# Node degrees from bfloat16 halves in four column tiles, in a four-layer graph network

## The chip, the cores and the metric

The kernel runs on one core of one Trainium2 chip. The metric is the time of one execution on the device in microseconds, the median of several runs. One profiled execution gives the trace that the views are read from.

## The reference

Four graph layers work on the same 2048x2048 adjacency of zeros and ones (with ones on its diagonal), each followed by a residual and a layer normalization over 64 features; the batch is 8. Cut to what matters here:

```python
deg = jnp.maximum(adj.sum(-1), 1.0)[:, None]                       # layer 0
industry = jnp.einsum('nm,bmf->bnf', adj / deg, x @ W_ind)
...
A_td = A + jnp.eye(n); deg = jnp.sum(A_td, axis=1)                 # layer 1
A_hat = rsqrt(deg)[:, None] * A_td * rsqrt(deg)[None, :]
H = jnp.einsum('bmd,nm->bnd', X, A_hat)
```

Layer 0 also has an attention over hyperedges, mixed with `industry` by a second attention. Layers 2 (Chebyshev supports and a learned one) and 3 (three message steps) use the adjacency as it is.

## The kernel before, in words

The adjacency's transpose stays in SBUF for the whole run, as 16 tiles `adj[t]` of 128 rows in two halves of 1024 columns, marked float32r (a 32-bit word that TensorE takes in one pass). `adj_c(t, c)` is one of four chunks of 512 columns; chunks 0 and 1 lie in the left half, 2 and 3 in the right. POOL issues the loads (`load_adj`, L211): the left halves during the setup, the right halves two in each of the first eight slots of the slot stage (`to_load`, L787). The halves of tiles 0 to 6 and 15 are called adj in the profile, those of tiles 7 to 14 adj_more.

Products with the adjacency are 128x512 matmuls. The features are split into a rounded part and a rest (`v0h`, `v0l` and so on), so each product takes two. Features come as four pairs of batches p; g is the half of the columns. `products()` is a generator that issues one matmul (`ug`) and yields; after the pair p = 0, g = 0 it runs `degrees(0)` and `degrees(1)` (L346), 64 matmuls with a square of ones (`du`), which sum the columns; each is followed by a yield. `inverses()` then makes `dinv` and the inverse degrees from `deg4`.

This generator is the *filler*. `fill(n)` calls it n times between other work, so that TensorE has something to do there. First come the setup and 20 calls; then the **slot stage** (the attention over hyperedges): 16 tiles of nodes with 12, 5, 5, 4 and fewer slots each, 57 in all. A slot is three matmuls into `pz`, `fill(5)`, on VectorE L793, L797 and L802 with an exponential on ScalarE (L795) between the first two, and an addition on POOL (L803). `pz` has three buffers. Each tile but the last begins with `fill(3)` and the coefficients of the next one.

Then comes the **mix stage**, 16 steps of one pair and one chunk each. A step has scores (`pf`, four tanh), an end (`pt`, transposes of `ind`, then the normalization), `pi` and `pg` of the next step, and a weighing (`pd`, a tanh, then `ind` by L937), with a `fill` of 8 or 9 after each. When the products of layer 0 have run out, the filler goes on with `layer1(p)` (`u`). That needs its input as `part[p, c]`: chunk c of pair p has to be through its mix step and normalized, read back, scaled and cast. Until then the filler yields "wait": the call puts no matmul on TensorE and only advances the `tick` counters that place delayed work. After the mix stage there are 96 more calls around the preparation of layer 2 (`pb`), and a loop drains what the filler still has (L1134); then the learned support starts (`ua`).

Matmuls, the adjacency's loads and everything passed to `pin` keep their program order on their engine; the place of other instructions is chosen by a planner when the program is built.

In layer 3 `check()` (L1686) tests 64 times, one block of 128x512 each, whether the adjacency survived the rounding: ScalarE casts a block read anew from HBM (L1689), VectorE counts what differs (L1690). If anything was counted, a general kernel would run after this one.

Of the kernel before, what the change touches and what calls it, by code (L numbers as in the profile page):

```python
# [30 lines left out]
F32 = mybir.dt.float32  # L31
F32R = mybir.dt.float32r
BF16 = mybir.dt.bfloat16
# [4 lines left out]
ALU = mybir.AluOpType  # L38
# [18 lines left out]
def tile_gnn_fast(  # L57
# [24 lines left out]
    nc = tc.nc  # L82
# [3 lines left out]
    P = 128  # L86
    NT = N // P
    NP = B // 2
    C = 512
    NCH = N // C  # L90
# [8 lines left out]
    def cols(c, n=C):  # L99
        return slice(c * n, (c + 1) * n)  # L100
# [3 lines left out]
    def evacuate(dst, src):  # L104

        turn[0] ^= 1
        if turn[0]:
            nc.scalar.copy(dst, src)
        else:
            nc.vector.tensor_copy(dst, src)  # L110
# [60 lines left out]
    def mm(*args, **kw):  # L171
        tc.keep_in_program_order(nc.tensor.matmul(*args, **kw))  # L172

    def transpose(dst, src):
        tc.keep_in_program_order(nc.tensor.transpose(dst, src, ident))  # L175
# [6 lines left out]
    ones = const.tile([P, P], F32, name="ones")  # L182
# [17 lines left out]
    hy = hy_scope.enter_context(tc.tile_pool(name="hy", bufs=1))  # L200
# [12 lines left out]
    def adj_c(t, c):  # L213

        return adj[t][c // 2][:, cols(c % 2)]
# [3 lines left out]
        block = adj_c(t, t // JT)[:, cols(t % JT, P)]  # L219
        eng.tensor_tensor(block, block.bitcast(F32), ident, op)  # L220

    ones_r = hy.tile([P, P], F32R, name="ones_r")
    nc.vector.tensor_copy(ones_r, ones)
    number = hy.tile([P, 12], F32, name="number")
    for i in range(12):
        nc.gpsimd.memset(number[:, i:i + 1], -1.0 - i)
# [1 line left out]
    deg4 = hy.tile([P, C], F32, name="deg4")  # L228
# [82 lines left out]
    def later(n, f):  # L311

        pending.append([n, f])
# [7 lines left out]
    def tick():  # L321
        for e in pending + soon:
            e[0] -= 1
        while pending and pending[0][0] <= 0:
            pending.pop(0)[1]()
        for e in [e for e in soon if e[0] <= 0]:
            soon.remove(e)
            e[1]()
# [13 lines left out]
    def products():  # L342

        deg1 = hy.tile([P, NT], F32, name="deg1")

        def degrees(g):  # L346
            du = pph.tile([P, 2, C], F32, tag="ph", name=f"du{g}", bufs=2)
            for t in range(NT):
                for i in range(2):
                    mm(  # L350
                        du[:, i, :], lhsT=ones_r, rhs=adj_c(t, 2 * g + i), start=t == 0, stop=t == NT - 1
                    )
                    yield
            for i in range(2):
                c = 2 * g + i
                r = slice(c * P // NCH, (c + 1) * P // NCH)
                evacuate(deg4[r, :], du[r, i, :])

        def inverses():

            pdc = places["small"]([P, JT, P], "pdc")
            for j in range(JT):
                transpose(pdc[:, j, :], deg4[:, cols(j, P)])
            pdc = pdc.rearrange("p j (c r) -> p c j r", c=NCH)[:, :, :, 0]
            d1 = deg1.rearrange("p (c j) -> p c j", c=NCH)
            nc.vector.tensor_scalar(d1, pdc, 1.0, None, op0=ALU.add)
            nc.gpsimd.tensor_tensor(dinv, deg1, neg_half[:, :NT], ALU.pow)
            nc.vector.tensor_scalar(d1, pdc, 1.0, None, op0=ALU.max)
            nc.vector.reciprocal(deg1, deg1)
            for _ in range(20):  # L370
                yield
            for c in range(NCH):
                pt = places["small"]([P, C], "pinv")
                for j in range(JT):
                    k = c * JT + j
                    transpose(pt[:, cols(j, P)], deg1[:, k:k + 1].to_broadcast([P, P]))
                row = va.tile([P, C], F32, tag="ut", name="inv", bufs=2)
                nc.scalar.copy(row, pt)
                nc.sync.dma_start(inv_hbm[:, cols(c)], row)
                for _ in range(4):  # L380
                    yield

        for p in range(NP):
            for g in range(2):
                own = (2 * g, 2 * g + 1)
                ug = pph.tile([P, 2, C], F32, tag="ph", name="ug", bufs=2)
                u = {c: ug[:, c % 2, :] for c in own}
                turning = inverses() if p == 0 and g == 1 else iter(())
                for t in range(NT):
                    for i in range(2):  # L390
                        for c in own:
                            mm(
                                u[c], lhsT=part[t // JT][i][:, t % JT, :], rhs=adj_c(t, c),
                                start=t == 0 and i == 0, stop=t == NT - 1 and i == 1,
                            )
                            tick()
                            if t > 1:
                                next(turning, None)
                            yield
                    if p == NP - 1 and g == 1 and t % JT == JT - 1:  # L400
                        first_parts(t // JT, free)
                    if p + 1 < NP and t % JT == JT - 1:
                        c = t // JT
                        if g == 1:
                            parts(p + 1, c)
                        if g == 1 and c < 2 or g == 0 and c >= 2:
                            fetch(p + 1, (c + 2) % NCH)
                if p == NP - 1:

                    for t in range(g * NT // 2, (g + 1) * NT // 2):  # L410
                        onto_diagonal(t, nc.gpsimd, ALU.add)
                for c in own:
                    ut = va.tile([P, C], F32, tag="ut", name="ut", bufs=2)
                    nc.scalar.copy(ut, u[c])
                    nc.sync.dma_start(u0_hbm[p][:, cols(c)], ut)
                if p == 0 and g == 0:
                    yield from degrees(0)
                    yield from degrees(1)

    def fill(n):  # L420
        for _ in range(n):
# [12 lines left out]
    pph = ph_scope.enter_context(tc.tile_pool(name="ph", bufs=1, space=PSUM))  # L434
    with tc.tile_pool(name="pa_ps", bufs=1, space=PSUM) as pps:
# [60 lines left out]
        for b in range(2):  # L496
# [21 lines left out]
            flat, lhsT=tri, rhs=oh.rearrange("p t b -> p (t b)"), start=True, stop=False  # L518
        )
        for t in range(NT - 1):  # L520
            nc.tensor.matmul(
                flat[:, (t + 1) * BINS:], lhsT=ones_b,
                rhs=oh[:, t:t + 1, :].to_broadcast([P, NT - 1 - t, BINS]), start=False, stop=False,
            )
        nc.tensor.matmul(
            flat, lhsT=ones_b, rhs=gtb[:, None, :].to_broadcast(bins), start=False, stop=True
# [17 lines left out]
        for t in range(NT // 2):  # L544
            for k in range(2):
                r = slice(k * E, (k + 1) * E)
# [50 lines left out]
        for t in range(NT):  # L597
            ph = pph.tile([P, 2, C], F32, tag="ph", name="ph", bufs=2)
            for p in range(NP):
                nc.tensor.matmul(  # L600
                    ph[:, p // 2, (p % 2) * 2 * (F + 2):(p % 2 + 1) * 2 * (F + 2)], lhsT=xt[t][:, p, :],
                    rhs=bd66.rearrange("p b f -> p (b f)"), start=True, stop=True,
# [33 lines left out]
            for k in range(2):  # L636
                nc.tensor.matmul(
                    pagg[k * E:(k + 1) * E, 0:G * (F + 1)], lhsT=m_n[:, t, :], rhs=ex[:, k].rearrange("p g c -> p (g c)"),
                    start=t == 0, stop=t == NT - 1,
# [415 lines left out]
    for i in range(steps + 1):  # L1055
        k = 9 if i > NCH else 8
# [403 lines left out]
    h = [None] * NCH  # L1460
# [110 lines left out]
    h = [None] * NCH  # L1571
# [21 lines left out]
    for u in range(2, UNITS):  # L1593
        c, k = divmod(u, 2)
# [82 lines left out]
    left = l2.tile([P, NT, NCH], F32, tag="m", name="left")  # L1677
    left_d = l2.tile([P, NT], F32, name="left_d")
    checks = [(t, k) for t in range(NT) for k in range(NCH)]
    seen_a = fcav.rearrange("p i b f -> p (i b f)")  # L1680
# [5 lines left out]
    def check():  # L1686
        t, k = checks.pop(0)
        ar = va.tile([P, C], F32R, tag="ut", name="ar", bufs=2)
        nc.scalar.copy(ar, seen_a)  # L1689
        nc.vector.scalar_tensor_tensor(  # L1690
            ar.bitcast(F32), seen_a, 1.0, ar.bitcast(F32), op0=ALU.mult, op1=ALU.not_equal,
            accum_out=left[:, t, k:k + 1],
        )
        if t // JT == k:

            block = seen_a[:, cols(t % JT, P)]
            one, two, same = (ar[:, cols(i, P)] for i in range(3))
            nc.vector.tensor_tensor(one, block, ident, ALU.add)
            nc.vector.tensor_tensor(two.bitcast(F32), one.bitcast(F32), ident, ALU.subtract)
            nc.vector.scalar_tensor_tensor(  # L1700
                same.bitcast(F32), two.bitcast(F32), 1.0, block, op0=ALU.mult, op1=ALU.not_equal,
                accum_out=left_d[:, t:t + 1],
            )
        if checks:
            load_check()
        else:

            nc.vector.tensor_reduce(wrong[:, 4:5], left.rearrange("p t k -> p (t k)"), AX.X, ALU.add)
            nc.vector.tensor_reduce(wrong[:, 6:7], left_d, AX.X, ALU.add)
            nc.vector.tensor_reduce(total, wrong, AX.X, ALU.add)  # L1710

            def add_up():
                pl = lps.tile([1, 1], F32, tag="mm", name="pl", bufs=4)
                mm(pl, lhsT=total, rhs=ones[:, 0:1], start=True, stop=True)
                nc.vector.tensor_copy(bad, pl)

            later(40, add_up)
# [66 lines left out]
    for p in range(NP):  # L1784
# [3 lines left out]
        for step in range(STEPS):  # L1788
# [4 lines left out]
            for g in range(2):  # L1793
# [16 lines left out]
                for mine in ([[c] for c in own] if very_end else [own]):  # L1810
                    for t in range(NT if p or step else 0):
                        if checks and t in (2, 7, 12):
                            check()
                        for i in range(2):
                            for c in mine:
                                mm(
                                    u[c], lhsT=x_part[t // JT][i][:, t % JT, :], rhs=adj_c(t, c),
                                    start=False, stop=t == NT - 1 and i == 1,
# [15 lines left out]
        h = h_next  # L1834
# [749 lines left out]
```

## Time and profile before

| | |
|---|---|
| median of 3 runs | 1757.61 us (1756.46 to 1757.87) |
| the profiled execution | 1757.78 us, of which 1756.0 are the span of its instructions |
| mean granted TensorE clock | 0.982 |
| setup, to the first slot | to about 68 us |
| slot stage | about 68 to 225 us |
| mix stage | about 225 to 480 us |
| preparation of layer 2 and drain | to 516 us |
| layers 2 and 3 | to the end; layer 3's checks from 1319 to 1721 us |

The views are: busy time by engine, groups of instructions by line, the chain of waits that ended last, timelines of one engine, and busy time by stage. A line of a timeline has the start in us, the duration, the engine, the line of the kernel, the operation and its tiles, the count, and in brackets the idle time before it with its releaser. A matmul's duration there is its latency; what it costs in a row is the distance between starts.

### The profile page before, as it was taken

How to read it: one execution, taken by the hardware profiler on the slowest of the kernel's cores; microseconds unless marked ns; L12 is line 12 of the kernel's file. 1: busy time of each engine (PE TensorE's matmuls, PEld its weight loads, DVE VectorE, ACT ScalarE, POOL GpSimd, SP SyncE). 2: the span in 40 equal slices, each digit the busy share in tenths (PEclk: the TensorE clock that was granted, in tenths of full speed). 3: DMA queues.
4: the chain of work that ended last, by engine and by line, in shares of the span. 5: the costliest groups of instructions: out<-in, count | busy, mean ns of one | idle time of the engine just before them, and what ended most of it. 6: DMA issues, size and time to landing. Idle time of an engine off the chain costs nothing.

```text
span 1756.0 us, 28202 instructions
## 1 busy us (share of the span) xinstructions
PE 1670.1 (95%) x11196; PEld 1212.3 (69%) x11196; DVE 858.7 (49%) x1583; ACT 600.9 (34%) x1123; POOL 572.2 (33%) x515
## 2 busy tenths in 40 slices
PE   6889899999899999999999999999989999999996
PEld 4657666666664444478788877777767877878775
DVE  7678945778642221210146168888623433433332
ACT  1345533344222212112223178888502222222221
POOL 4578845556534443422023001313310200202001
PEclk9899999999999999999999999999999999999998
DMA  9744334444330000027244557675571111211211
GB/s 327 254 159 124 104 130 144 144 144 144 111 121 6 30 31 1 24 82 288 104 144 132 123 125 159 132 159 127 150 257 40 52 57 46 61 42 43 60 42 39
DMA packets 171182, 195.84 MB, mean 112 GB/s; under 512 B 71536, under 2 KB 116336, under 8 KB 169760
## 3 DMA queue, kind: packets, MB, share of 16 engines
q1 hardware_dynamic: 160096, 154.54, 30.3%
q0 software_dynamic: 8544, 30.68, 5.2%
q10 hardware_dynamic: 2400, 8.72, 1.4%
q8 instruction: 90, 1.47, 0.4%
q14 instruction: 52, 0.43, 0.1%
HBM read 126.72 MB, written 67.17 MB: 110 GB/s over the span
## 4 chain that ended last, share of the span: by engine, by line
PE 75%; DMA 4%; DVE 3%; POOL 2%; issue 2%; ACT 1%; SPq 1%; POOLq 0%; ACTq 0%; DVEq 0%
PE u L172 38%; PE ua L172 13%; PE py L172 7%; PE pw L172 5%; PE ug L172 3%; PE pr L172 2%; PE pf L172 1%; PE po L172 1%; PE pt L175 1%; DMA adj_more<-adj_hbm 1%; DVE w_half L1490 1%; PE s L172 1%; DMA est<-est_hbm 1%; PE pd L172 1%; PE pi L172 1%
## 5 line engine op out<-in xcount | busy, mean ns | idle before, releaser
L172 PE MATMUL ua<-pt,xn 128*128 128x512 f32 x512 | 230.2, 592 | 1.4 <-DVE pt L1150 1.4
L1488 ACT COPY w_half<-pw 128x512 f32<-128x512 f32 x316 | 191.5, 688 | 44.4 <-PE pw L172 43.4
L172 PEld LDWEIGHTS ua<-pt,xn 128*128 128x128 f32 x512 | 96.9, 190 | 111.1 <-issue 104.0
L1490 DVE COPY w_half<-pw 128x512 f32<-128x512 f32 x196 | 134.0, 716 | 72.2 <-PE pw L172 69.5
L172 PE MATMUL py<-w_half,xg 128*32 128x128 f32 x4096 | 144.1, 282 | 2.9 <-ACT w_half L1488 2.2
L172 PE MATMUL u<-adj,v0h 128*128 128x512 f32 x384 | 134.2, 427 | 1.1 <-ACT h L1779 1.1
L172 PEld LDWEIGHTS py<-w_half,xg 128*32 128x32 f32 x4096 | 112.7, 139 | 20.7 <-ACT w_half L1488 2.5
L172 PE MATMUL u<-adj_more,v2h 128*128 128x512 f32 x384 | 125.4, 405 | 0.0
L172 PE MATMUL u<-adj,v0l 128*128 128x512 f32 x384 | 124.6, 402 | 0.0
L172 PE MATMUL u<-adj_more,v2l 128*128 128x512 f32 x384 | 124.1, 400 | 0.0
L172 PE MATMUL pw<-est,wst 64*128 64x256 f32 x1024 | 117.5, 321 | 4.2 <-DMA est<-est_hbm 2.1
L1156 POOL TENSOR_TENSOR acc<-acc,pt 128x512 f32<-128x512 f32 x60 | 76.5, 1276 | 104.2 <-DVE pt L1150 103.5
L172 PEld LDWEIGHTS pw<-est,wst 64*128 64x128 f32 x1024 | 81.7, 187 | 36.1 <-issue 18.8
L1150 DVE TENSOR_SCALAR pt<-pt 128x512 f32<-128x512 f32 x64 | 29.7, 464 | 152.8 <-ACT pt L1149 152.6
L1661 POOL TENSOR_TENSOR x<-x,rows 128x512 f32<-128x512 f32 x16 | 22.7, 1438 | 234.2 <-PE pt L175 208.8
L1689 ACT CAST ar<-fcav 128x512 fp32r<-128x512 f32 x64 | 39.5, 618 | 167.1 <-DMA fcav<-in_adj_t 166.1
L1149 ACT ACTIVATE pt<-s 128x512 f32<-128x512 f32 x64 | 38.0, 598 | 164.7 <-PE s L172 164.7
L1690 DVE SCALAR_TENSOR_TENSOR ar<-fcav,ar 128x512 f32<-128x512 f32 x64 | 44.6, 697 | 101.2 <-ACT ar L1689 101.2
L172 PE MATMUL u<-adj,v1h 128*128 128x512 f32 x288 | 93.7, 403 | 0.0
L172 PE MATMUL u<-adj_more,v3h 128*128 128x512 f32 x288 | 93.4, 402 | 0.0
L172 PE MATMUL u<-adj_more,v3l 128*128 128x512 f32 x288 | 93.4, 400 | 0.0
L172 PE MATMUL u<-adj,v1l 128*128 128x512 f32 x288 | 92.1, 397 | 0.0
(405 smaller groups left out, 3224.4 us busy)
## 6 DMA issues: line engine op xcount, KB each, us to landing
fcav<-in_adj_t SPq DMA_DIRECT2D x64, 256.0 KB, 2.9
u_hbm<-ut SPq DMA_DIRECT2D x48, 256.0 KB, 3.5
xg<-u_hbm SPq DMA_DIRECT2D x24, 512.0 KB, 6.9
adj<-in_adj_t POOLq DMA_DIRECT2D x16, 512.0 KB, 8.3
adj_more<-in_adj_t POOLq DMA_DIRECT2D x16, 512.0 KB, 8.9
adj_hbm<-adj_more SPq DMA_DIRECT2D x16, 512.0 KB, 6.2
x_hbm<-r SPq DMA_DIRECT2D x28, 256.0 KB, 2.6
hs_hbm<-st ACTq DMA_DIRECT2D x8, 584.0 KB, 3.6
```

The costliest lines, as they stand in the source:

```text
L172: tc.keep_in_program_order(nc.tensor.matmul(*args, **kw))
L175: tc.keep_in_program_order(nc.tensor.transpose(dst, src, ident))
L1149: nc.scalar.activation(pt, s, AF.Exp)
L1150: nc.vector.tensor_scalar(pt, pt, 1.0, None, op0=ALU.max)
L1156: nc.gpsimd.tensor_tensor(accs[c], accs[c], pt, ALU.add)
L1488: pin(nc.scalar.copy(dst, src))
L1490: pin(nc.vector.tensor_copy(dst, src))
L1661: nc.gpsimd.tensor_tensor(xs, xs, b2.to_broadcast([P, JT, P]), ALU.add)
L1689: nc.scalar.copy(ar, seen_a)
L1690: nc.vector.scalar_tensor_tensor(ar.bitcast(F32), seen_a, 1.0, ar.bitcast(F32), op0=ALU.mult, op1=ALU.not_equal, accum_out=left[:, t, k:k ...
```

## The change

The sums of the columns are made from the upper 16 bits of each word of the adjacency, read as bfloat16 with a step of two elements; a bfloat16 is the upper half of a float32, and zeros and ones are exact in it. The ones have 32 columns for each chunk, and chunk c is written to the partitions 32c to 32c+31 of one PSUM bank, so each matmul uses a quarter of TensorE's columns. All four chunks of a tile are summed in one pass over t, with a yield after every second tile: 8 yields of 8 matmuls in place of 64 of one. One copy of 128 partitions fetches the result where four of 32 did. The test in layer 3 rounds to bfloat16 in place of float32r.

```diff
-    ones_r = hy.tile([P, P], F32R, name="ones_r")
-    nc.vector.tensor_copy(ones_r, ones)
+    ones_h = hy.tile([P, P], BF16, name="ones_h")
+    nc.vector.memset(ones_h, 1.0)
...
-        def degrees(g):
-            du = pph.tile([P, 2, C], F32, tag="ph", name=f"du{g}", bufs=2)
+        def degrees():
+
+            du = pph.tile([P, 2, C], F32, tag="ph", name="du", bufs=2)
             for t in range(NT):
-                for i in range(2):
-                    mm(
-                        du[:, i, :], lhsT=ones_r, rhs=adj_c(t, 2 * g + i), start=t == 0, stop=t == NT - 1
-                    )
+                for c in range(NCH):
+                    r = slice(c * P // NCH, (c + 1) * P // NCH)
+                    top = adj_c(t, c).bitcast(BF16).rearrange("p (n h) -> p n h", h=2)[:, :, 1]
+                    mm(du[r, 0, :], lhsT=ones_h[:, r], rhs=top, start=t == 0, stop=t == NT - 1)
+                if t % 2:
                     yield
-            for i in range(2):
-                c = 2 * g + i
-                r = slice(c * P // NCH, (c + 1) * P // NCH)
-                evacuate(deg4[r, :], du[r, i, :])
+            evacuate(deg4, du[:, 0, :])
...
                 if p == 0 and g == 0:
-                    yield from degrees(0)
-                    yield from degrees(1)
+                    yield from degrees()
...
         ar = va.tile([P, C], F32R, tag="ut", name="ar", bufs=2)
-        nc.scalar.copy(ar, seen_a)
+        short = ar.bitcast(BF16)[:, 0:C]
+        nc.scalar.copy(short, seen_a)
         nc.vector.scalar_tensor_tensor(
-            ar.bitcast(F32), seen_a, 1.0, ar.bitcast(F32), op0=ALU.mult, op1=ALU.not_equal,
-            accum_out=left[:, t, k:k + 1],
+            short, seen_a, 1.0, short, op0=ALU.mult, op1=ALU.not_equal, accum_out=left[:, t, k:k + 1],
         )
```

## The prediction

> **What bounds the kernel now.** The engine table and the slices come first, then the chain of waits, then the timelines of PE and POOL around the degrees, then the DMA slices, then busy time by stage.
>
> ```profile
> PE 1670.1 (95%) x11196; PEld 1212.3 (69%) x11196; DVE 858.7 (49%) x1583; ACT 600.9 (34%) x1123; POOL 572.2 (33%) x515
> ```
>
> PE is 95% busy, so a matmul taken away looks like time won. But the lost 5% sits in few places, and one of them is where the change lies. Three answers show it (start us, duration us, engine, line, operation, tiles, count, [idle before it <- releaser]):
>
> ```profile
> 89.86 1.10 PE L172 MATMUL du<-adj,ones_r 128*128 128x512 f32 x4
> 92.03 0.47 PE L172 MATMUL pz<-hrh,ident_r 128*128 128x512 f32 x1 [1.07 <-DVE y L797]
> ...
> 94.44 0.47 PE L172 MATMUL pz<-hrh,ident_r 128*128 128x512 f32 x1 [0.30 <-DVE y L797]
> ...
> 105.30 0.62 PE L172 MATMUL du<-adj,ones_r 128*128 128x512 f32 x2
> ```
> ```profile
> 82.35 0.54 POOL L211 DMA_DIRECT2D adj_more<-in_adj_t  x1
> ...
> 94.01 0.56 POOL L211 DMA_DIRECT2D adj_more<-in_adj_t  x1
> 94.56 0.54 POOL L211 DMA_DIRECT2D adj<-in_adj_t  x1
> ```
> ```profile
> DMA to landing us min/median/max: 8.3/8.4/8.5
> ```
>
> The degree matmuls run from 89.9 to 119 us, 233 ns apart (five in 94.98 to 96.84 with three pz beside them). Those of the right half of the adjacency begin at 105.3. The right half is still being loaded before that: its last load is issued at 94.56 and lands 8.4 us later (the last line, from the view of tile adj, 60 to 125 us), at **103.0**; the DMA slices of 92 to 108 us show the engines full until 101 and empty from 103. So today nobody waits for these loads, and only because the left half's sums go first.
>
> Busy time by stage (PE, PEld, DVE, ACT, POOL, then clock, DMA share, GB/s):
>
> ```profile
> 150.00:220.00 70.00, 61.35 (x261) 46.49 (x260) 65.26 (x113) 40.55 (x105) 61.30 (x48) 0.98 0.33 105
> 240.00:450.00 210.00, 207.69 (x929) 134.87 (x927) 143.04 (x193) 84.06 (x145) 118.28 (x94) 1.00 0.44 141
> 485.00:516.00 31.00, 31.00 (x142) 25.17 (x143) 14.76 (x31) 6.28 (x13) 8.13 (x5) 0.91 0.49 151
> 1319.00:1750.00 431.00, 422.30 (x2006) 336.80 (x2004) 159.51 (x357) 93.75 (x157) 44.76 (x28) 1.00 0.17 49
> ```
>
> In the slot stage (to 220 us) VectorE is 93% busy and PE only 88%; in the mix stage (240 to 450) PE is the bound at 99%, again in the drain of the filler (485 to 516) and in layer 3. Matmuls are worth their time in the last three, not in the first.
>
> **What the Trainium skill says.** "TensorE: Matmul & The Clock Gate", Part 3, "Measured speedup vs the span model": matmuls on different column tiles run at once, 2.38 times for three. The trace agrees for two: the two products of pd (128*64) take 1.01 us in the chain, one pi of the same 512 columns 0.86; and 32 py of 128 columns in four tiles take 1.05 us, 33 ns each. The same page, Part 1: after a window of about 3.4 us with an idle array the clock is halved until a busy window has passed. The trace agrees: after 5.6 us of waiting at 478.9 us, matmuls are 0.43 us apart until 491. "SBUF — State Buffer", "Door 1: The DMA port swizzle", counts up to 8 bfloat16 elements as a stride without penalty; here it is 2, and no row of this trace reads so.
>
> **The change part by part.** One `next` on the filler is a *call*. The calls are fixed by the code: 20 before the slots, 57 slots of 5 and 15 tiles of 3 make 350 up to the mix; mix step 0 starts its scores at 406, then steps of 32 and, from 5, of 36 calls; 963 end the mix, 96 more follow, and the rest is drained. The filler gives 4x2x64 = 512 products and 64 degree matmuls, one a call, then 512 of layer 1: 1088. After the change the degrees take 8 calls of 8 matmuls. So every later product comes **56 calls earlier**.
>
> (a) *The sums themselves.* 64 x 233 ns = 14.9 us become 16 groups of four. Lower bound 233 ns a group, 3.7 us; upper, by py's 33 ns for 128 columns, 4 x 4 x 33 = 530 ns, 8.5 us. I take 3.7. It matters little, because of (b).
>
> (b) *A new wait.* The degrees begin at the same place as before, call 65 in slot 8 of tile 0 (89.9 us), but calls 65 to 68 now read tiles 0 to 7 in **both** halves, and calls 69 to 72, in slot 9, tiles 8 to 15. Tile 7's right half is issued at 82.35 and lands by about 92: slot 8 hardly waits. Tiles 8 to 15 land from 93 to 103.0, so PE stands in slot 9 until 103.0; before, it was in slot 10 at 94.44. Slot 10's three pz are queued behind that; VectorE's L793, ScalarE's exponential and POOL's accumulation wait for them. With the four last sums and one product at half clock (0.43 us each), slot 10 starts at about 104: **+9.5**. Half clock for half of the next two slots costs 1.5 more. The loads themselves cannot be hurried: DMA is full from 68 to 101 us.
>
> (c) *What the slots give back.* Two VectorE copies of deg (0.69 each) go; one 128x512 ScalarE copy takes the place of two of 0.58: -1.4 where VectorE is the bound. The waits of 0.3 to 0.4 between slots vanish while VectorE has caught up: -1 (0 to -3, as VectorE's order, two slots behind, may stay). The 4.73 us that VectorE waits at 125.3 for POOL's dinv moves to slot 11 or so, where POOL has been idle and only its own 2.96 us count: -1.5. Sum of (b) and (c): 11 - 4 = **+7** (3.5 to 9.5). The 56 products that move into this stage cost 13.1 us of PE, the sums save 11.2; the 1.9 us lie under the wait for the loads.
>
> (d) *The mix stage.* Layer 1 now starts at call 521, not 577, and catches up with its inputs. Chunk (p, 3) is stored 17 calls after its mix_end and cast 22 later, at calls 574, 715, 859 for p = 0, 1, 2; layer 1 asks for it from 569, 703, 844 on. So 6 + 13 + 16 = **35 calls return "wait"** and put nothing on PE: 35 x 0.2335 = 8.2 us less between 240 and 450. This is a gain as far as the next mix matmul is ready. The critical pair is pd to pt: ind is written 2.5 to 6.5 us after pd starts (389.62+0.68 against 386.82; 437.9 against 431.43). Where nine waits fall between pf and pt, pt comes at 1.08 + 2.1 + 1.92 = 5.1 us after pd: mostly in time. I take -6.5 (0 to -8.2).
>
> (e) *The drain.* 56 - 35 = 21 products fewer at its end (29 become 8): -4.9, PE 100% busy there. Against that, two ends of layer 1 (0.69 + 0.69 + 0.69 on VectorE, 1.3 + 1.65 on POOL each) come 20 calls earlier, into the chain that PE already waits for at 459.7 (3.6 us) and 478.9 (5.6 us): +1.5 (0 to 3). Net **-3.4**.
>
> (f) *The test of layer 3, ones_h.* ScalarE's cast (620 ns) and VectorE's compare (692 ns) change only a type; were each twice as long, 64 x 1.3 = 84 us would lie under a PE that is 98% busy while VectorE is at 37% and ScalarE at 22%; were they half, nothing waits for them. If that cover went, a rectified h queued behind one compare would come up to 0.7 later. The memset in place of a copy of 128x128 is start-up work that no one waits for. Zero.
>
> Sum: +7 - 6.5 - 3.4 = -2.9, taken as -2.7, because the bound of (d) is the wider one and lies on the side of a loss. The profiled execution took 1757.78 (span 1756.0), 0.17 above the median of the runs shown: **1755.1 us**, from 1750 to 1760 if all goes this way. A measurement of this kernel tells 0.2%, 3.5 us, from no change.
>
> **The rivals.** *Slower: the holes in the mix stage are not filled.* With 9 waits in a row PE reaches pt before ind, stands, and half clock follows; (d) is then 0 and the time 1757.78 + 7 - 3.4 = 1761.4, or 1764 with (b) at its upper end. It decides once less than a tenth of the 8.2 us is kept at +7. For it: VectorE busy 55.12 of 70 us in 380 to 450, two ready times of 5.4 and 6.5 us; against: PE has waited only 1.5 us in the whole of 335 to 380. Chance 0.25.
>
> *Faster: VectorE's order changes.* If the planner, seeing the wait, lets VectorE finish slots 8 and 9 during it (2 x 1.4 us) and no dinv wait remains, the stage loses 3.5, and with (d) and (e) whole: 1757.8 + 3.5 - 6.5 - 4.9 = 1750. For: only work kept in program order has a fixed place; against: today's order sits two slots behind without need. 0.13.
>
> *The tiles do not overlap.* 64 x 233 ns again: 7.5 us in slot 8, 7.5 in slot 9, so slot 10 starts at 105.6 in place of 104, with a warm clock: about 1756. The py and pd rows speak against. 0.06.
>
> **How the numbers follow.** The likeliest, 0.56, splits 0.25 faster, 0.25 same, 0.06 slower, its centre lying just inside the limit of 1754.1. The slower rival gives 0.05 same and 0.20 slower; the faster one 0.12 and 0.01; the last 0.02 same, 0.04 slower. Sum: faster 0.37, same 0.33, slower 0.30. From 1748 to 1764 covers all cases but their tails.
>
> **What would show it.** Right: du as 128*32 x64, the last near 103.4; PE idle some 9 us before it with a DMA load of adj as releaser; the first pi at about 239.5 (232.5 now); 35 products fewer between first pi and pb; the first ua near 515.5 (518.2). Wrong: no wait for DMA at 93 to 103; PE idle over 2 us more in 240 to 450; checks of layer 3 that hold up PE.

## The result, and the profile after

The changed kernel takes **1774.24 us** (median of 4 runs, 1772.53 to 1776.97) against 1757.74 for the kernel before in the same comparison: a ratio of **1.0093, interval 1.0079 to 1.0108**. It is slower by 16.5 us, where the prediction had 1755.1 and a range that ended at 1764. The profiled execution took 1772.79, of which 1771.0 are its span, 15.0 more than before.

The row of the page with the busy time of each engine:

```profile
PE 1666.9 (94%) x11196; PEld 1205.3 (68%) x11196; DVE 848.1 (48%) x1581; ACT 601.4 (34%) x1122; POOL 568.2 (32%) x515
```

PE has as many instructions as before and is busy for 3.2 us less, and the kernel is 15 us longer: PE stands still for 18 us more. The starts of the first instructions of each part, in us, say where:

| from | to | before | after | difference | predicted |
|---|---|---|---|---|---|
| start | first pz (setup) | 68.4 | 65.9 | -2.5 | 0 |
| first pz | first pi (slot stage) | 164.1 | 165.5 | +1.4 | +7 |
| first pi | first pb (mix stage and a little more) | 252.4 | 274.6 | **+22.2** | -6.5 |
| first pb | first ua (drain) | 33.3 | 25.8 | -7.5 | -3.4 |
| first ua | end | 1237.8 | 1239.2 | +1.4 | 0 |

The first row is not counted as an effect: in the profiled executions of all kernels here the setup ends between 65.1 and 70.4 us. Busy time by stage in the kernel after (PE, PEld, DVE, ACT, POOL, clock, DMA share, GB/s), the same stretches as in the prediction:

```profile
150.00:220.00 70.00, 60.60 (x266) 46.26 (x266) 68.45 (x118) 40.24 (x104) 60.63 (x50) 1.00 0.31 99
240.00:450.00 210.00, 187.71 (x796) 119.15 (x797) 119.91 (x183) 75.48 (x128) 102.97 (x83) 0.94 0.40 132
485.00:516.00 31.00, 26.45 (x117) 21.12 (x116) 17.85 (x32) 8.36 (x15) 11.52 (x8) 0.86 0.62 212
1319.00:1750.00 431.00, 429.87 (x2031) 342.17 (x2030) 160.51 (x358) 94.59 (x159) 40.97 (x26) 1.00 0.18 54
```

In the slot stage VectorE has even less air than before: 68.45 of 70 us. In the mix stage PE, once 99% busy, is idle for 22 of 210 us, and its clock is 0.94. The prediction had named more than 2 us of idle time there as the sign that it was wrong. PE alone from the first pi to the first pb, before and then after:

```profile
232.50:484.90 252.40, 240.89 (x1070) 0.99 0.43 139
```
```profile
231.40:506.00 274.60, 244.86 (x1035) 0.94 0.39 128
```

There are 35 matmuls fewer, just the number that the prediction had counted, worth 8.2 us. But the idle time rose from 11.5 to 29.7 us (+18.2), and the 35 fewer took 4.0 us *more* of busy time, so matmuls at half clock cost 4.0 + 8.2 = 12.2. Together 18.2 + 12.2 - 8.2 = 22.2.

What PE waited for between 225 and 520 us, before and then after (engine, line, releaser: us in total, times, longest):

```profile
PE pb L172 <- DMA xn<-x_hbm: 5.6, 1, 5.6
PE pt L175 <- DVE ind L937: 3.6, 1, 3.6
PE ua L172 <- DVE pt L1150: 1.4, 1, 1.4
...
```

```profile
PE u L172 <- ACT v3h L167: 14.5, 3, 6.4
PE u L172 <- ACT v2h L167: 7.3, 2, 4.5
PE pg L175 <- DMA gn<-gs_hbm: 4.1, 1, 4.1
PE po L172 <- ACT ut L1033: 3.8, 2, 1.9
```

The first two lines of after, 21.8 us in five waits, are not in the list of before at all. They are matmuls of layer 1, that is, of the **filler**, and they wait for the cast of their own input. PE's timeline around the longest one:

```profile
370.22 0.63 PE L175 MATMUL pt<-ident,ind 128*128 128x128 f32 x4
377.22 1.22 PE L172 MATMUL u<-adj_more,v3h 128*128 128x512 f32 x2 [6.37 <-ACT v3h L167]
378.34 1.22 PE L172 MATMUL u<-adj_more,v3l 128*128 128x512 f32 x2
379.36 0.63 PE L172 MATMUL u<-adj_more,v3h 128*128 128x512 f32 x1
379.79 1.50 PE L172 MATMUL pi<-ut,fcav 128*128 128x512 f32 x2
```

After pt nothing runs for 6.4 us; then layer 1's u comes first, at half clock (two of them in 1.12 us from start to start, at 233 ns each it would be 0.47), and only behind it the mix stage's own pi. The chain of waits shows what u had waited for (start us, us, what):

```profile
367.11 1.64 POOL ln_r L860
...
368.78 0.70 DVE r L863
...
369.50 2.09 DMA x_hbm<-r
...
371.99 3.35 DMA y<-x_hbm
...
375.48 1.04 POOL y L970
...
376.55 0.63 ACT v3h L167
...
377.22 0.79 PE u L172
```

It is the whole way of a chunk from its mix step into layer 1: normalized, stored, loaded again, scaled by POOL, cast by ScalarE.

**Why the filler does not yield "wait" there.** `part[p, c]` is entered in the function `cast` that `l1_parts` hands to `after(16, scale, 6, cast)`. It is entered when the cast is *issued*, 22 ticks behind the load's issue, and not when its data is there. In the kernel before, the counts of the code leave 22 to 27 calls between the issue of the cast of chunk 2 or 3 and the first matmul that needs it. In the changed kernel they leave 1 call for chunk 3 of p = 0, 1 and 2, and 5 to 11 calls for chunk 2.

For chunk 3, empty calls make it worse. Twenty-two ticks stand for time only while most of them put a matmul on PE (22 x 0.2335 = 5.1 us); a call that yields "wait" ticks as well and takes none. Layer 1 has run out of inputs, so 6, 13 and 16 of the 22 calls ahead of the three casts are empty. The cast goes into ScalarE's queue, and the very next call puts the matmul that needs it on PE. The two waits for v2h come without any empty call: a lead of 5 calls was too short by itself. The first of them, and the half clock behind it:

```profile
427.34 0.63 PE L172 MATMUL u<-adj_more,v1l 128*128 128x512 f32 x2
430.69 0.50 PE L172 MATMUL u<-adj_more,v2h 128*128 128x512 f32 x1 [2.73 <-ACT v2h L167]
431.03 1.02 PE L172 MATMUL pi<-ut,fcav 128*128 128x512 f32 x2
...
433.09 1.05 PE L172 MATMUL u<-adj_more,v2l 128*128 128x512 f32 x2
```

Matmuls keep their program order, so in both cases the mix stage's own matmuls stand behind the one that waits.

### The profile page after: what moved, and what is told of

Its sections match the earlier page's. It is cut to its first block, busy times and chain, and to the rows that moved or that the text cites. A ratio compares the mean times of both kernels' runs of the same rounds, so it can differ in the third digit from the quotient of the medians.

```text
span 1771.0 us, 28173 instructions
## 1 busy us (share of the span) xinstructions
PE 1666.9 (94%) x11196; PEld 1205.3 (68%) x11196; DVE 848.1 (48%) x1581; ACT 601.4 (34%) x1122; POOL 568.2 (32%) x515
## 3 DMA queue, kind: packets, MB, share of 16 engines
q1 hardware_dynamic: 160096, 154.54, 29.7%
## 4 chain that ended last, share of the span: by engine, by line
PE 72%; DMA 5%; DVE 5%; POOL 4%; issue 2%; ACT 1%; SPq 1%; POOLq 0%; DVEq 0%; ACTq 0%
PE u L172 36%; PE ua L172 12%; PE py L172 7%; PE pw L172 5%; PE pr L172 2%; PE ug L172 2%; PE po L172 1%; POOL ln_r L860 1%; DMA y<-x_hbm 1%; DMA adj_more<-adj_hbm 1%; PE pf L172 1%; DVE w_half L1488 1%; PE s L172 1%; PE pt L175 1%; DMA est<-est_hbm 1%
## 5 line engine op out<-in xcount | busy, mean ns | idle before, releaser
L172 PE MATMUL u<-adj_more,v2h 128*128 128x512 f32 x384 | 126.5, 409 | 7.3 <-ACT v2h L167 7.3
L1659 POOL TENSOR_TENSOR x<-x,rows 128x512 f32<-128x512 f32 x16 | 22.2, 1405 | 236.2 <-PE pt L175 210.3
L1688 ACT CAST ar<-fcav 128x512 bf16<-128x512 f32 x64 | 39.5, 617 | 167.9 <-DMA fcav<-in_adj_t 166.9
L1689 DVE SCALAR_TENSOR_TENSOR ar<-fcav,ar 128x512 bf16<-128x512 f32 x64 | 44.9, 701 | 102.6 <-ACT ar L1688 102.6
```

The lines of the kernel that those rows point to most:

```text
L1659: nc.gpsimd.tensor_tensor(xs, xs, b2.to_broadcast([P, JT, P]), ALU.add)
L1688: nc.scalar.copy(short, seen_a)
L1689: nc.vector.scalar_tensor_tensor(short, seen_a, 1.0, short, op0=ALU.mult, op1=ALU.not_equal, accum_out=left[:, t, k:k + 1],)
```

## The experiments

Ratios are to the runs of the kernel before in the same comparison, with a 95% interval; medians in us. Stage times are those of each kernel's profiled execution.

**1. 56 empty calls behind the sums**, so that layer 1 is as late as before:

```diff
                     yield from degrees()
+                    for _ in range(56):
+                        yield
```

> The changed kernel with 56 empty calls of the filler after the sums, so that every later product has its old place again. Theory A (the loss comes from the filler running 56 calls ahead, so that layer 1 catches up with the mix stage and waits for it at the head of TensorE's queue): the waits for v2h and v3h go, and the time is 1752 to 1760. Theory B (the sums themselves, with their wait for the adjacency's loads at 92 to 101 us and the lower clock after it): the loss stays, 1772 or more, since the sums are the same. Theory C (layer 3's test): 1772 or more as well.

1763.98, ratio 1.0044 (1.0028 to 1.0060). The waits for v2h and v3h are gone; first pi to first pb takes 253.6 us, as before. So the advance is their cause. But 7.5 us of loss are left, and they are in another place: the slot stage takes 172.2 us. What VectorE waited for there (70 to 225 us):

```profile
DVE pz L793 <- PE pz L172: 15.5, 11, 6.3
...
DVE deg L367 <- POOL dinv L366: 5.4, 1, 5.4
```

Against 8.9 and 4.7 us in the kernel before. This half of the expectation was missed.

**2. The old sums in the new order**, an edit of the kernel before: full-width float32r sums with the square of ones, and the old test, but all four chunks in one pass over t and 8 yields in place of 64:

```diff
-                for i in range(2):
+                for c in range(NCH):
                     mm(
-                        du[:, i, :], lhsT=ones_r, rhs=adj_c(t, 2 * g + i), start=t == 0, stop=t == NT - 1
+                        du[c // 2][:, c % 2, :], lhsT=ones_r, rhs=adj_c(t, c), start=t == 0, stop=t == NT - 1
                     )
+                if t % 2:
                     yield
...
```

> The kernel before (full-width sums of float32r words, its own test in layer 3), but with the 64 sums given in 8 calls of 8, so that the products come 56 calls earlier as in the changed kernel. Theory A: the mix stage has the same waits for v2h and v3h, some 22 us, and the time is 1770 to 1785 (the 11 us of sums that the changed kernel saves are spent here, mostly under the wait for the loads). Theory B: little of the loss, 1757 to 1765. Theory C: 1757 to 1760.

1781.89, ratio 1.0134 (1.0113 to 1.0155), with the same waits of PE in the mix stage:

```profile
PE u L172 <- ACT v3h L167: 14.2, 3, 6.1
PE u L172 <- ACT v2h L167: 7.3, 2, 4.5
```

Neither bfloat16 nor the column tiles are needed for these waits. The number of yields is enough: first pi to first pb takes 274.4 us, as in the changed kernel. The slot stage takes 172.3 us, 8.2 more than before, with the 11 us of sums that this kernel does not save.

**3. and 4. The test of layer 3 alone, and the sums alone.** The kernel before with the new test; the changed kernel with the old one:

```diff
-        nc.scalar.copy(ar, seen_a)
+        short = ar.bitcast(BF16)[:, 0:C]
+        nc.scalar.copy(short, seen_a)
...
```

> The kernel before with the new test of layer 3 alone. Theories A and B: within 2 us of before, 1756 to 1760, as TensorE is 98% busy while the test runs. Theory C: most of the 16.5 us, 1770 or more.

> The changed kernel with the old test of layer 3: the sums alone. Theories A and B: as the changed kernel, 1772 to 1777. Theory C: 1757 to 1760.

1758.71, ratio 1.0007 (0.9998 to 1.0015), and 1777.24, ratio 1.0112 (1.0091 to 1.0133). All of the loss is in the sums. The two rows of the test in the page of the changed kernel (count, busy us, mean ns, idle time before):

```profile
L1688 ACT CAST ar<-fcav 128x512 bf16<-128x512 f32 x64 | 39.5, 617 | 167.9 <-DMA fcav<-in_adj_t 166.9
L1689 DVE SCALAR_TENSOR_TENSOR ar<-fcav,ar 128x512 bf16<-128x512 f32 x64 | 44.9, 701 | 102.6 <-ACT ar L1688 102.6
```

With float32r, in the page of the kernel before, they take 618 and 697 ns: the narrower type costs and brings nothing here.

**5. One call fewer in each slot**, the other way to take the advance back: 57 slots with 4 calls in place of 5.

```diff
-                fill(5)
+                fill(4)
```

> The changed kernel with four filler calls in a slot in place of five: 57 calls fewer before the mix stage, so its products lie against the mix stage where they lay before, and the slot stage has 57 matmuls less. Theory A (the loss is the stock of filler work used up too early): no waits for v2h or v3h, mix stage as before; slot stage not longer than before; 1748 to 1759. Theory B (the wait of the sums for the loads costs the 7.5 us that e1_pad56 still lost): the mix stage is well, the slot stage 6 to 9 us longer, 1761 to 1768.

1757.80, ratio 1.0006 (0.9996 to 1.0017). The waits for v2h and v3h are 0, the slot stage takes 163.3 us (164.1 before), first pi to first pb 253.0 (252.4). Of 150 us from 70 on, PE is busy 122.9 where it was 130.2. The edit does one thing more: the sums come later, at 92.3 to 99.6 us, and wait for the loads for only 0.4 us; experiment 7 shows that this alone does not undo the loss. So with the filler in step again the loss is gone, and the 11 us of TensorE that the sums save are worth nothing: they lie in a stage that VectorE bounds.

**6. The chunk is marked ready 12 ticks later**; the filler stays ahead.

```diff
-            part[p, c] = split(va, y, f"v{c}", 1, [P, JT, P], pin=True)
+            made = split(va, y, f"v{c}", 1, [P, JT, P], pin=True)
+            after(12, lambda: part.update({(p, c): made}))
```

> The changed kernel, where a chunk counts as ready for layer 1 only 12 calls after its cast was issued; nothing else is moved, and the filler says wait 47 times in place of 36. Theory A1 (the loss comes from a matmul that stands at the head of TensorE's queue, waiting for its cast, with the mix stage's own matmuls behind it): those matmuls go ahead, the waits for v2h and v3h fall from 22 us to under 6, and the time is 1758 to 1768. Theory A2 (the mix stage's chain is too long for the work that is left, whoever stands first): the waits turn up at pt, pd, pf or pg, and the time stays within 4 us of the changed kernel, 1770 to 1778.

1762.90, ratio 1.0030 (1.0020 to 1.0041): 11 us regained with the order of the sums untouched. The wait for v2h is gone, that for v3h is 8.2 us: 12 ticks are too few. By the counts, all calls between the cast of chunk 3 and its first matmul are empty ones for p = 0, 1 and 2.

**7. The sums one half-product later** (behind p = 0, g = 1, the inverses one further), when all of the adjacency is there:

```diff
-                turning = inverses() if p == 0 and g == 1 else iter(())
+                turning = inverses() if p == 1 and g == 0 else iter(())
...
-                if p == 0 and g == 0:
+                if p == 0 and g == 1:
                     yield from degrees()
```

> The changed kernel with the sums after the second column half of the first pair (64 calls later, when all of the adjacency has landed), the inverses moved behind them. The mix stage still gets its products 56 calls early, so its 22 us of waits stay. If the wait for the loads at 92 to 101 us costs what e1_pad56 still lost, the time is 1764 to 1770; if VectorE's backlog covers it, as the slot stage of the changed kernel (1.4 us longer only) suggests, 1771 to 1777.

1774.97, ratio 1.0112 (1.0088 to 1.0137). The sums wait for no load any more (they run from 126.5 to 132 us), and the time does not move. So to be rid of the new wait for the loads, which was the prediction's one large cost, gains nothing in the changed kernel: the slot stage takes 168.5 us without it. v3h and v2h wait 14.2 and 8.9 us.

**8. and 12. Fewer empty calls, and empty calls elsewhere**: 28 in the place of experiment 1's 56; then 56 behind p = 0, g = 1, after the inverses.

> The changed kernel with 28 empty calls after the sums, half of the advance. By the counts 7 calls of the filler say wait in place of 35. Theory A1 or A2: the waits for v2h and v3h are 3 to 9 us in place of 22, and the time is 1764 to 1770, near that of e1_pad56. If the loss went with the advance in equal steps instead, about 1769.

> As e1_pad56, but with the 56 empty calls after the second column half of the first pair, behind the inverses, which so run right after the sums as in the changed kernel. If e1_pad56 lost its 7.5 us because the inverses with VectorE's wait for dinv came at their late place again, after the wait for the loads, then this one has a slot stage like the changed kernel's, 163 to 167 us from the first pz to the first pi in place of 172, and 1755 to 1760. If 56 calls without a matmul lose the time themselves (the clock, or the planner's order), it stays at 1762 to 1768.

1764.50, ratio 1.0029 (1.0015 to 1.0043), and 1764.42, ratio 1.0040 (1.0026 to 1.0055). With 28 the waits in the mix stage are half gone (7.0 and 4.5 us, once each, in the slowest of its runs; 3 to 9 us had been expected), and the runs spread from 1757.1 to 1768.5. In the other place the slot stage takes 172.2 us as in experiment 1. That the empty calls pushed the inverses to a bad place was the idea, and it fell.

**9. and 10. Four calls in the slots but five in the first slot of each tile**, without and with the chunk marked ready 8 ticks later:

```diff
-                fill(5)
+                fill(4 if s else 5)
```

> The changed kernel with five filler calls in the first slot of a tile and four in the others: 41 calls fewer before the mix stage in place of e5_fill4's 57, so 14 products are left for the drain in place of 30, and by the counts no call says wait. If the counts are enough, 16 x 0.2335 = 3.7 us less than e5_fill4: 1752 to 1756, faster than both kernels. If a lead of five calls over the casts is too small, TensorE waits for v2h or v3h again, 4 us or more, and the time is 1757 to 1763.

> e9_fill4_after_first with a chunk counted as ready 8 calls after its cast was issued (2 wait calls by the counts). If e9 still waits at v2h or v3h, this one doesn't, and is 2 to 5 us faster than e9: 1752 to 1757. If e9 has no such wait, the two are within 2 us.

1758.79, ratio 1.0010 (0.9999 to 1.0020), and 1756.97, ratio 1.0001 (0.9984 to 1.0019). Neither beats the kernel before. In their profiles v3h is waited for again, twice each, 7.6 and 5.9 us in all, which for the second was a miss; the runs spread from 1755.0 to 1766.9 and from 1752.6 to 1773.5. In experiment 9 no call is empty by the counts, and the longer of its waits, 6.3 us, comes with 9 calls between cast and matmul. That the wait differs from run to run would explain the spread; one profile of each can't show it.

**11. The chunk marked ready 24 ticks later** in the changed kernel.

> The changed kernel with 24 calls between cast and ready in place of e6_late_ready's 12 (59 wait calls in place of 47). Theory A1, blocking at the head of the queue: the 8 us that e6 still waited at v3h fall under 3, the 12 more calls left for the drain cost 2.8, and the time is 1757 to 1762. Theory A2 for the rest: the waits go over to pf, pt and pg, and the time is that of e6 or more, 1762 to 1768.

1756.38, ratio 0.9996 (0.9987 to 1.0005). The whole loss is gone with the late mark alone, and sums, calls and the wait for the loads are those of the changed kernel. PE's waits in the mix stage begin with another one now:

```profile
PE pf L172 <- DVE ind L883: 8.0, 3, 3.4
```

This is near the slower rival of the prediction: with layer 1 held back, empty calls follow one another and PE reaches pf before VectorE has written ind. It is 8.0 us here, less than the 21.8 that it takes the place of.

**13. and 14. Both remedies, and the late mark in the kernel before**: 24 ticks with the slots of experiment 9; 24 ticks in the kernel before.

> e9_fill4_after_first with a chunk counted as ready 24 calls after its cast. If stock and readiness add up, the slot stage is that of e9 and the mix stage that of e11_late_ready_24: no waits for v2h or v3h over 1 us, 1750 to 1756, faster than both kernels. If readiness alone does all, as in e11: 1755 to 1759.

> The kernel before with the same late readiness. In it no matmul waits for a cast, so Theory A1 expects no gain: 1756 to 1764 (the later readiness makes some calls say wait, whose products go to the drain). If late readiness is a gain of its own and not the cure of this change, it is faster than before by 3 us or more, 1749 to 1755.

1750.89, ratio 0.9961 (0.9946 to 0.9976), and 1752.08, ratio 0.9964 (0.9951 to 0.9978). Both are faster than the kernel before by 6 to 7 us, and so than the changed one, and they cannot be told from each other. The second was a miss: the kernel before was thought to have nothing to gain from the mark, since no wait for v2h or v3h is in its list. Where its gain comes from is open; in the profiled executions first pi to first ua is 3.0 us shorter (282.7 for 285.7), half of the gain. That is within the spread of runs: experiment 3, whose program is the kernel before's there, has 289.3.

**15. The 56 empty calls spread**, one behind every fourth product:

> As e1_pad56, with the 56 empty calls spread, one after every fourth product that follows the sums. If a row of 56 calls without a matmul is what lengthened the slot stage of e1_pad56 and e12_pad_behind_inverses to 172 us, it is 163 to 168 us here and the time 1756 to 1760. If the wait of the sums for the loads did it, the slot stage stays at 171 or more and the time at 1762 to 1767.

1767.95, ratio 1.0053 (1.0039 to 1.0068); the slot stage takes 172.8 us. It is not the row of empty calls that costs in experiment 1. A stage of 171 us or more had been expected here if the wait of the sums for the loads is what costs.

## Why the prediction was wrong

**Step (d) failed**, with the sign. Its count was right: 35 calls yield "wait", and 35 matmuls are missing. It took an entry in `part` for data that is there, and asked only whether the *mix stage* could use the gap ("as far as the next mix matmul is ready"). It did not ask what stands at the head of PE's queue when the gap ends. The working has the cast 22 calls behind the store, and layer 1 asking for the chunk 5, 12 and 15 calls ahead of the cast: the calls from there on are empty, and the matmul follows the cast by one call. For chunk 2, which the working does not name, no call is empty, but the lead has shrunk from 26 or 27 calls to between 5 and 11, and two of the five waits are there.

In place of -6.5 it is about +22 (the stretch of the table has the start of the next part in it): 18.2 of idle PE and 12.2 of halved clock, less the 8.2 of the matmuls that are gone. Of the 12.2 most lie behind the five waits: PE runs at half clock for 3.4 to 6.3 us after each of them, and once more after the 4.1 us for gn. Experiments 1, 2, 5, 6 and 11 show the cause from both sides: the waits come with the lead alone, and go when the lead or the early mark goes.

How much of the 16.5 us it is can only be estimated. Against the kernel before, the late mark takes the changed kernel from 1.0093 to 0.9996, some 17 us, and the kernel before from 1 to 0.9964, some 6. If the mark has the same gain of its own in both, about 11 are this blocking. The remaining 4 to 6 us are still there when both kernels have the mark, 0.9996 against 0.9964, and their place and cause are open. Experiment 13, with the mark and a smaller lead, has no such remainder (0.9961), but it differs in two ways: its sums also wait for the loads for only 1.6 us, where those of experiment 11 wait for 6.3. In the profiles it is not the stretch from first pi to first ua that is longer in experiment 11 than in 14 (280.0 against 282.7), in spite of the 8.0 us that pf waits for ind, but the slot stage (167.4 against 163.8); the profile of 11 is that of its fastest execution, though.

**Step (b) was right in place and nearly in size, and step (c) gave back more of it than was said.** The sums around the loads in the changed kernel:

```profile
89.00 1.77 PE L172 MATMUL du<-adj,ones_h 128*32 128x512 bf16 x28
...
91.09 0.47 PE L172 MATMUL pz<-hrh,ident_r 128*128 128x512 f32 x1
...
98.18 0.62 PE L172 MATMUL du<-adj_more,ones_h 128*32 128x512 bf16 x4 [1.52 <-DMA adj_more<-in_adj_t]
...
101.28 0.61 PE L172 MATMUL du<-adj,ones_h 128*32 128x512 bf16 x2 [0.65 <-DMA adj<-in_adj_t]
...
102.41 0.63 PE L172 MATMUL pz<-hrh,ident_r 128*128 128x512 f32 x1
```

The last load released them at 101.3 (predicted 103.0) and slot 10 began at 102.4 (104), at half clock as said. Slot 10 starts 11.3 us behind slot 9, where it was 2.4 before: a hole of some 9 us, 6.0 of them PE's idle time until the loads. But VectorE used the time:

```profile
93.99 0.68 DVE L795 SCALAR_TENSOR_TENSOR y<-pz,y 128x512 f32<-128x512 f32 x1
...
95.97 0.68 DVE L795 SCALAR_TENSOR_TENSOR y<-pz,y 128x512 f32<-128x512 f32 x1
...
103.93 0.70 DVE L791 TENSOR_TENSOR pz<-pz,R 128x512 f32<-128x512 f32 x1 [5.93 <-PE pz L172]
```

Of the hole of some 9 us VectorE stood for 5.9, because the planner had put the later operations of slots 8 and 9 into it; before, these came two slots later. That was the premise of the faster rival. With the shorter wait for dinv (3.7 for 4.7 us) and VectorE 98% busy later on, the stage lost 1.4 us in this profile in place of 7. Experiments 4, 6 and 11, whose slot stage has the same code, have 168.0, 168.3 and 167.4 us, a loss of 3.3 to 4.2. So this term was mis-sized by 3 to 6 us, on the safe side.

What the same wait costs when PE does less in the stage is another matter. In experiments 1, 12 and 15 the slot stage is 8 to 9 us longer than before, and the sums wait for the loads for 6.1 to 7.9 us. Experiment 5 has as little PE work there as experiment 1 (122.9 of 150 us from 70 on, in both) but only 0.4 us of this wait, and its stage is not longer (163.3). That speaks for the wait as part of the cause. But the changed kernel has the wait as well, with a stage of 165.5, and experiment 2 has 172.3 without it. Why it costs more with the empty calls stays open, since the planner's order on VectorE differs from one program to the next.

**Step (e)**: the drain lost 7.5 us, not 3.4. The 21 products are -4.9. The other 2.6 are about what the kernel before lost when it began this stretch at half clock (0.54 from 484.9 to 491.3 us) behind its wait for pb, which the changed kernel does not have; this is argued from the two profiles, and no experiment tests it. And the loss of 1.5 in the chain ahead of it can't be told apart from (d).

**Steps (a) and (f)** were right: the sums do overlap in the column tiles, and the test costs nothing that can be told from zero (experiment 3, 0.9998 to 1.0015). The rival without overlap is out. The **slower rival** had the side and the stage, but not the mechanism: no pt waits for ind in the changed kernel.

## What to carry to other kernels

Filler work in an in-order queue should not be issued before its data is certain to be there: one matmul that waits holds up all that stand behind it. A count of calls is a measure of time only while the calls do work, so where "ready" is set by a count, look whether it is entered at the issue or at the end of the last step, how many calls lie between it and the first use, and what happens once the calls are empty. And taking matmuls out of a stage that another engine bounds is no gain (11 us of them were worth 0 here), while the stock of filler that they leave, used up earlier, must be paid for in the stage that PE bounds.

## What was not expected of the hardware

Four column tiles of 32 overlap wholly here, for 512 columns of bfloat16 read with a step of two elements. The view of tile du in the changed kernel (count: ns min/median/max, first and last start):

```profile
L172 PE MATMUL du<-adj,ones_h x32: 386/388/610, 89.0 to 101.3; 128*32 128x512 bf16 x32
L172 PE MATMUL du<-adj_more,ones_h x32: 385/398/610, 90.6 to 100.0; 128*32 128x512 bf16 x32
```

In the timeline above 28 of them start between 89.00 and 90.60, when the next four follow: 57 ns each, 229 for a group of four, against 233 for one full-width product. In the Trainium skill, "TensorE: Matmul & The Clock Gate", Part 3, gives 2.38 times for three tiles; four gave 4.1 here, and no cost of the step of two is to be seen, for which the trace of before had no row.

Part 1 of that page, on the halved clock behind an idle window, explains why a stall costs more than itself: in the stretch from first pi to first pb 18.2 us more of idle time came with 12.2 us of slow matmuls. The page has the window at about 3.4 us. In this trace a stall of 2.73 us, at 430.69, was enough: the clock granted from 432.0 to 435.5 us is 0.52.
